# An attention kernel on one core: PSUM as four pairs of banks, keys and queries in alternating units, and a norm spread over steps

## The chip, the core and the metric

The kernel runs on one NeuronCore of a Trainium2 chip. A core has TensorE (PE: matmuls and, as PEld, weight loads), VectorE (DVE), ScalarE (ACT), GpSimd (POOL), and SyncE (SP), which here issues the DMAs. Matmuls write to PSUM[...]; DVE and ACT read PSUM and write to SBUF, the working memory. Each engine runs its own instructions in order and waits on semaphores for the others. The metric is the device time of one execution, in microseconds, as the median of several runs.

## What is computed

The input is 16 images of 64 x 64 positions with 256 channels, in fp32. There are two layers, each with a group norm over 32 groups of 8 channels ahead of it and a residual around it:

```python
# layer 0: linear attention over all positions of an image, 8 heads of 32
q, k, v = split(gn(x) @ w_qkv)
q = softmax(q, over the 32 channels of a head) * 32**-0.5
k = softmax(k, over all positions)
x = x + ((k.T @ v).T @ q per head) @ w_out
# layer 1: local attention in a 7 x 7 window, 8 heads of 32
q, k, v = gn(x) @ Wq + bq, gn(x) @ Wk + bk, gn(x) @ Wv + bv
scores = q . (k at each of the 49 neighbours + emb)    # emb: by row for heads 0-3, by column for 4-7
x = x + sum over neighbours of softmax(scores) * v
```

## The kernel before

**Layout.** An image is kept channels first, as two halves of 128 channels by 4096 positions. The positions are cut into eight strips of 512. Strips 1 to 7 are blocks of 8 columns by 64 rows, strip 0 holds the two borders of the image (5 columns on one side, 3 on the other). The tuple KEYED lists the strips with the border last, ORDER lists them as layer 0 visits them, and UNITS lists the four units of 16 columns that the local attention visits, unit 0 last. The 16 images follow each other in one program; each engine of TensorE, ACT, DVE and SP carries out its instructions in the order in which the Python code writes them.

**PSUM.** There are two double tiles of two banks (`double`, in the profile pd) and four single ones (`single`, ps); lines 366 to 387. `psum2` hands out the two doubles in turn, `bank` the first half of the next one. `banks` hands out, again in turn, double 0, double 1, singles 0 and 1, singles 2 and 3, with the engine that is to empty each of the two banks (0 is DVE, 1 is ACT).

**Layer 0** (`layer0`, line 515). For 16 pieces of 256 positions, queries and keys are made (L531), put through exp by ACT (L535), summed and transposed by DVE (L538, L562), and the context is accumulated in singles 0 and 1 (L549). At the end the context is multiplied by the output weights and with the queries (L642), two channel halves in turn; DVE adds the result to the image (L653, L656) and takes the statistics of the sum (L465).

**Preparing layer 1** (line 1023 on). `group_stats` turns statistics into mean and rstd in three steps, with two tiny matmuls that average over a group (L262 to L281). The weights are scaled with rstd (L668), and the mean is folded into the biases (`fold_bias`, and L1036 with L1039 for the values). `positional_products` (L695) and `positional` (evacuations L686 by DVE, L684 by ACT) make the products of queries with the position embedding; `store_rings` and `load_rings` bring them through DRAM into rows of the query tile qq. `values` (line 734) makes the values of one strip: eight matmuls (L743), an add of the bias by DVE (L746), a store to the scratch vpad in DRAM (L751; the border, L756, takes eight DMAs). After the last strip `load_window` (L804, four DMAs each) brings the values of the first two units back, as windows.

**Keys and queries** (`keys_queries`, line 760). This is done for the first four heads (hg 0) and, after their local attention, for the others (hg 1); I call each a half of the layer. First the keys of four pairs of strips in the order of KEYED, (2,3), (4,5), (6,7), (1,0), then the queries of the same pairs. Each pair takes eight matmuls (L771) into two banks, and each strip is evacuated one head at a time, by 32 x 512 instructions (for the border 32 x 320 and 32 x 192), keys into kaug, queries into qq. The queries of (1,0) are held back by a `yield`: they are made in the first step of the local attention.

**Local attention** (`local_attention`, line 807) goes through 20 groups (four units with five groups of at most two chunks of keys) in 24 steps. At its start four tiny matmuls (L951) write to all four banks of the doubles. A step makes the scores of its group (L834, into a double from `psum2`), whose exp ACT writes to work tiles (L843 for hg 0, L846 for hg 1); it multiplies the exps of the group of the step before with the values (`weighted`, L878, into singles 0 and 1, `outs`), and sums those of the group before that (`summed`, L908, into singles 2 and 3, `zs`). DVE adds the parts of neighbouring chunks (`both_chunks`, L863). When a unit is complete, ACT copies `outs` (L970), DVE transposes `zs` (L915) and inverts the sums in `finish`, POOL multiplies and adds to the image (L934, L942), SP stores.

**Between the steps** the callbacks `between0` and `between1` do the next image's work. Step n calls them with the group of step n - 2. In hg 1 `between1` starts the loads of the next image's first channel half after the first group, takes two strips' statistics (L465, DVE) after each of the first four groups of the second unit, makes the three steps of `group_steps` after the first three groups of the third unit (with the matmul of the mean in the score bank that comes next, `next_bank`), and normalises two strips (L285, two instructions each) after the second and third group of the last unit.

**Work tiles.** One pool of six buffers of 128 x 1024 serves layer 0's exps, the values before they are stored, and the exps of the scores, in turn.

## Time and profile before

| | |
|---|---|
| median of 3 runs | 5888.22 us |
| lowest, highest | 5876.85, 5892.97 us |
| the profiled execution, its own time | 5892.37 us |
| its span, first to last instruction | 5890.5 us |
| mean granted clock of TensorE | 0.954 |
| instructions | 169110 |

In the lines that follow, a row of the timeline gives start, length, engine, line, operation, output <- inputs with the shape, and the number of instructions that it merges; in brackets stands how long the engine had been idle before it, and what ended that. A row of the waits gives who waited for whom, the total in us, the number of times and the longest. A row of a group gives line, engine and operation, shape, count, then busy us and mean ns of one, then the idle time before them and what ended most of it. In the chain, shares are of the span. The time of one image is about 367 us: layer 0 and the preparation of layer 1 take some 165 of them, each half of layer 1 some 100.

### The profile page before, as it was taken

What the parts mean: (1) busy time and instruction counts of PE and PEld (TensorE: products, weight loads), DVE (VectorE), ACT (ScalarE), POOL (GpSimd) and SP (SyncE); (2) the same over time, 40 slices, a digit from 0 to 9 for tenths busy, and PEclk for the clock granted to TensorE, in tenths of its full rate; (3) what the DMA queues carried; (4) which work ended last, traced back from release to release, by engine and by line L of the source; (5) the groups of instructions that cost most, each with busy time, mean ns of one, the idle gap of its engine ahead of it and who ended that gap; (6) DMA issues with size and microseconds to landing.
All of it is one profiled execution on the core that took longest, in us unless ns stands there. A gap on an engine that the chain in (4) does not pass through costs nothing.

```text
span 5890.5 us, 169110 instructions
## 1 busy us (share of the span) xinstructions
PE 5235.4 (89%) x75313; PEld 3609.8 (61%) x75313; DVE 3439.0 (58%) x5946; ACT 2193.7 (37%) x3089; POOL 1335.2 (23%) x1946
## 2 busy tenths in 40 slices
PE   7889898898998989989889998988989989899997
PEld 4656566566665666656656666565665666656665
DVE  4565655656565565655655556565574655656555
ACT  1341624425144251442514325144351433514335
POOL 3031231302212022130221302213032130321303
PEclk9999999999999999999999999999999999999999
DMA  4543616445173451734517345173451734517344
GB/s 121 107 102 56 133 54 116 101 74 119 42 130 96 76 115 35 131 94 77 117 33 131 94 77 117 33 133 92 79 119 32 136 86 81 114 35 135 87 77 86
DMA packets 751604, 540.80 MB, mean 92 GB/s; under 512 B 241408, under 2 KB 682368, under 8 KB 748416
## 3 DMA queue, kind: packets, MB, share of 16 engines
q1 hardware_dynamic: 750864, 529.89, 44.1%
q8 instruction: 592, 9.70, 0.7%
q14 instruction: 148, 1.21, 0.1%
HBM read 371.04 MB, written 158.73 MB: 90 GB/s over the span
## 4 chain that ended last, share of the span: by engine, by line
PE 77%; DVE 8%; ACT 5%; issue 5%; DMA 2%; SPq 1%; POOL 1%; DVEq 0%; ACTq 0%; POOLq 0%
PE pd L531 15%; PE pd L834 13%; PE ps L878 8%; PE pd L771 7%; PE ps L549 6%; PE ps L771 5%; ACT qq L684 4%; PE ps L642 4%; PE pd L743 4%; PE pd L642 4%; PE ps L743 4%; PE ps L908 4%; DVE e L863 3%; PE ps L695 2%; DMA vpad<-v 1%
## 5 line engine op out<-in xcount | busy, mean ns | idle before, releaser
L863 DVE TENSOR_TENSOR e<-e,e 128x384 f32<-128x384 f32 x1024 | 732.4, 742 | 773.1 <-PE ps L878 615.2
L834 PE MATMUL pd<-qq,kaug 64*64 64x112 f32 (+4 forms) x27648 | 938.0, 277 | 159.8 <-issue 71.1
L834 PEld LDWEIGHTS pd<-qq,kaug 64*64 64x64 f32 x27648 | 813.2, 139 | 319.5 <-issue 181.8
L531 PE MATMUL pd<-wqkv,img 128*128 128x512 f32 x2048 | 948.8, 608 | 3.2 <-DVE img L285 3.2
L443 POOL TENSOR_TENSOR others<-others,rc 128x32 f32<-128x32 f32 x128 | 32.1, 251 | 2858.6 <-DVE rc L919 2858.4
L535 ACT ACTIVATE eq<-pd 128x1024 f32<-128x1024 f32 x256 | 261.9, 1023 | 1077.7 <-PE pd L531 1077.7
L531 PEld LDWEIGHTS pd<-wqkv,img 128*128 128x128 f32 x2048 | 399.1, 196 | 412.1 <-issue 376.6
L878 PE MATMUL ps<-e,vw 128*32 128x112 f32 (+1 forms) x18432 | 575.2, 261 | 65.2 <-issue 64.5
L538 DVE TENSOR_REDUCE qz<-eq 128x16 f32<-128x512 f32 x256 | 175.5, 686 | 766.9 <-ACT eq L535 766.9
L846 ACT ACTIVATE e<-pd 128x896 f32<-128x896 f32 (+2 forms) x576 | 461.4, 836 | 430.5 <-PE pd L834 423.5
L843 ACT ACTIVATE e<-pd 128x896 f32<-128x896 f32 (+2 forms) x576 | 462.4, 838 | 400.7 <-PE pd L834 395.8
L684 ACT ACTIVATE qq<-ps,bias 32x512 f32<-32x512 f32 (+2 forms) x512 | 318.6, 648 | 733.5 <-PE ps L695 668.6
L908 PE MATMUL ps<-e,ones 128*32 128x128 f32 (+2 forms) x10240 | 404.2, 266 | 146.3 <-DVE e L863 113.0
L878 PEld LDWEIGHTS ps<-e,vw 128*32 128x32 f32 x18432 | 419.0, 114 | 154.4 <-issue 117.5
L942 POOL TENSOR_TENSOR img<-img,r 128x320 f32<-128x320 f32 (+1 forms) x512 | 493.2, 993 | 0.0
L549 PE MATMUL ps<-xtok,eq 128*128 128x257 f32 x2048 | 483.4, 380 | 0.0
L549 PEld LDWEIGHTS ps<-xtok,eq 128*128 128x128 f32 x2048 | 387.4, 190 | 149.8 <-issue 107.1
L684 ACT ACTIVATE kaug<-pd,bias 32x512 f32<-32x512 f32 x256 | 173.7, 678 | 674.8 <-PE pd L771 671.9
L686 DVE TENSOR_SCALAR qq<-ps,bias 32x512 f32<-32x512 f32 (+2 forms) x416 | 312.3, 759 | 151.0 <-PE ps L771 145.2
L934 POOL TENSOR_TENSOR r<-r,r 128x512 f32<-128x512 f32 x256 | 340.7, 1352 | 140.5 <-DVE r L921 134.8
L908 PEld LDWEIGHTS ps<-e,ones 128*32 128x32 f32 x10240 | 253.3, 116 | 189.6 <-DVE e L863 148.1
L465 DVE BATCH_NORM_STATS2 st<-img 128x6 f32<-128x512 f32 x512 | 332.1, 679 | 9.7 <-DMA img<-in_xc 5.2
(128 smaller groups left out, 6609.9 us busy)
## 6 DMA issues: line engine op xcount, KB each, us to landing
vw<-vpad SPq DMA_DIRECT2D x512, 288.0 KB
img<-in_xc SPq DMA_DIRECT2D x256, 256.0 KB
xtok<-in_xt SPq DMA_DIRECT2D x64, 1024.0 KB
out<-img SPq DMA_DIRECT2D x256, 256.0 KB
vpad<-v SPq DMA_DIRECT2D x112, 512.0 KB
qq<-pos SPq DMA_DIRECT2D x128, 256.0 KB
qq<-in_ring SPq DMA_DIRECT2D x128, 256.0 KB
pos<-qq SPq DMA_DIRECT2D x128, 112.0 KB
```

What stands on the lines that cost most here:

```text
L531: nc.tensor.matmul(ps[:, t], xn[k][:, n0 : n0 + P], n.wqkv_sb[:, k, : 2 * C], start=(k == 0), stop=(k == 1))
L549: nc.tensor.matmul(pc[hg][:, : C + 1], eq[p][:, t, C + hg * P : C + (hg + 1) * P], xtok[p // 4][:, 2 * (p % 4) + t], start=(p == 0 and t = ...
L642: nc.tensor.matmul(py[a], w4[rows, h, hg, co * P : (co + 1) * P], qv[rows, 4 * hg + h, 8 * HD * i : 8 * HD * (i + 1)], start=(h == 0 and h ...
L684: nc.scalar.activation(dst, src, AF.Identity, bias=bias)
L743: nc.tensor.matmul(pi[:, t], x[k][:, n0 : n0 + P], wv[:, k], start=(k == 0), stop=(k == 1))
L771: nc.tensor.matmul(ps[a], wgt[:, k, hg * P : (hg + 1) * P], x[k][:, strip(pair[a])], start=(k == 0), stop=(k == 1),)
L834: nc.tensor.matmul(to, kaug[pl][rows, u, 8 * c : 8 * c + 8].rearrange("p r w -> p (r w)"), q, start=True, stop=True,)
L843: nc.scalar.activation(e.rearrange("p (a n) -> p a n", a=2), ps[:, :, : 2 * m], AF.Exp)
L863: nc.vector.tensor_tensor(part, part, rows_of(c - 1, before, r0, 8 * c), ALU.add)
L878: nc.tensor.matmul(dst, stationary, pr, **flags)
L908: nc.tensor.matmul(dst, ones, pr, start=True, stop=True)
L942: nc.gpsimd.tensor_tensor(yv, xv, by_rows(add[:, :, a - w0 : e - w0], xv), ALU.add)
```

## The change

The two double and four single tiles become four pairs of two banks each. `psum2` takes pairs 0 and 1 in turn, `outs` is pair 2 and `zs` pair 3, each emptied by one instruction (the copy by ACT, the transpose by DVE) in place of two. Layer 0's context uses the halves of pairs 2 and 3; both channel halves of its output are added by two wide DVE instructions. The values take the four pairs in turn and are evacuated by one add. The folds of the mean have banks of their own choice: pair 2 (second half), pair 1 (second half) and pair 1 (first half).

Keys and queries go by pairs of strips (0,1), (2,3), (4,5), (6,7), keys then queries of each pair; the pairs of banks are taken in turn, so that keys use pairs 0 and 2 and queries 1 and 3. DVE evacuates all keys, ACT all queries, except the last unit (queries of strips 6 and 7, behind the `yield`), whose heads are split between them. Where a pair holds no border, both strips go in one 32 x 1024 instruction for each head.

The windows of the first two units are loaded after the stores of strips 7 and 1, so one strip's store and the border's stand behind them on SP. For the next image's norm, `between1` takes one strip's statistics after each of eight groups from the fourth on, makes the steps of `group_steps` one group later than before, and normalises one half of one strip after each of the first four groups of the last unit. `group_steps` reads mean and variance where `bn_aggr` wrote them, without a copy.

The diff, cut; the old form of `keys_queries` and what only renames banks is left out:

```diff
--- before.py
+++ after.py
@@ -260,18 +261,16 @@
             nc.vector.bn_aggr(mv[:, k], stats[:, k].rearrange("p a b -> p (a b)"))
-        mean_c, var_c = mv[:, :, 0:1], mv[:, :, 1:2]
-        rhs = small.tile([P, 2, 1], F32, tag="gn1", name=f"gn1{name}")
-        nc.vector.tensor_copy(rhs, mean_c)
+        mean_c, var_c = mv[:, :, 0], mv[:, :, 1]
         yield
         pm = psum(f"pm{name}")
-        nc.tensor.matmul(pm[:, 0:2], self.grp, rhs.rearrange("p a b -> p (a b)"), start=True, stop=True)
+        nc.tensor.matmul(pm[:, 0:2], self.grp, mean_c, start=True, stop=True)
         mean = small.tile([P, 2], F32, tag="gnm", name=f"gnm{name}")
...
         d = small.tile([P, 2], F32, tag="gnd", name=f"gnd{name}")
-        nc.vector.tensor_tensor(d, rhs.rearrange("p a b -> p (a b)"), mean, ALU.subtract)
+        nc.vector.tensor_tensor(d, mean_c, mean, ALU.subtract)
         nc.vector.tensor_tensor(d, d, d, ALU.mult)
-        nc.vector.tensor_tensor(d, d, var_c.rearrange("p a b -> p (a b)"), ALU.add)
+        nc.vector.tensor_tensor(d, d, var_c, ALU.add)
         yield
...
@@ -363,28 +362,19 @@
 
-        double = [ps.tile([P, 2, 512], F32, tag=f"pd{i}", name=f"pd{i}") for i in range(2)]
-        single = [ps.tile([P, 512], F32, tag=f"ps{i}", name=f"ps{i}") for i in range(4)]
-        turn = [0, 0]
+        pairs = [ps.tile([P, 2, 512], F32, tag=f"pair{i}", name=f"pair{i}") for i in range(4)]
+        turn = [0]
 
...
             turn[0] += 1
-            return double[turn[0] % 2]
-
-        def banks():
-
-            i = turn[1] % 4
-            turn[1] += 1
-            if i >= 2:
-                return single[2 * i - 4 : 2 * i - 2], (0, 1)
-            return [double[i][:, j] for j in range(2)], (i, i)
+            return pairs[turn[0] % 2]
 
...
 
-            return double[(turn[0] + 1) % 2][:, 0, 64:]
+            return pairs[(turn[0] + 1) % 2][:, 0, 64:]
 
...
@@ -634,26 +624,22 @@
                 for co in range(2):
-                    py = [double[a // 2][:, a % 2, : 2 * P] if co else single[a][:, : 2 * P] for a in range(4)]
+                    py = [pairs[2 - 2 * co + a][:, :, : 2 * P] for a in range(2)]
                     for h in range(4):
...
                                 nc.tensor.matmul(
-                                    py[a],
+                                    py[a // 2][:, a % 2],
                                     w4[rows, h, hg, co * P : (co + 1) * P],
...
                     xv = x[co][:, s0 * 512 : (s0 + 2) * 512].rearrange("p (t a n) -> p a t n", a=4, n=HD)
-                    if co:
-                        for a in (0, 2):
-                            part = double[a // 2][:, :, : 2 * P].rearrange("p a (t n) -> p a t n", n=HD)
-                            nc.vector.tensor_tensor(xv[:, a : a + 2], part, xv[:, a : a + 2], ALU.add)
-                    else:
-                        for a in range(4):
-                            nc.vector.tensor_tensor(xv[:, a], py[a].rearrange("p (t n) -> p t n", n=HD), xv[:, a], ALU.add)
+                    for a in range(2):
+                        part = py[a].rearrange("p a (t n) -> p a t n", n=HD)
+                        nc.vector.tensor_tensor(xv[:, 2 * a : 2 * a + 2], part, xv[:, 2 * a : 2 * a + 2], ALU.add)
                     for s in (s0, s0 + 1):
...
@@ -733,17 +719,13 @@
 
-            pv, _ = banks()
+            pv = pairs[KEYED.index(s) % 4].rearrange("p i (t c) -> p (i t) c", c=C)
             v4 = work_tile(f"v4_{b}_{s}").rearrange("p (t c) -> p t c", c=C)
-            for i in range(2):
-                pi = pv[i].rearrange("p (t c) -> p t c", c=C)
-                for t in range(2):
-                    n0 = s * 512 + (2 * i + t) * P
-                    for k in range(2):
-                        nc.tensor.matmul(pi[:, t], x[k][:, n0 : n0 + P], wv[:, k], start=(k == 0), stop=(k == 1))
-            for i in range(2):
-                pi = pv[i].rearrange("p (t c) -> p t c", c=C)
-                nc.vector.tensor_tensor(v4[:, 2 * i : 2 * i + 2], pi, bv.unsqueeze(1).to_broadcast([P, 2, C]), ALU.add)
+            for t in range(4):
+                n0 = s * 512 + t * P
+                for k in range(2):
+                    nc.tensor.matmul(pv[:, t], x[k][:, n0 : n0 + P], wv[:, k], start=(k == 0), stop=(k == 1))
+            nc.vector.tensor_tensor(v4, pv, bv.unsqueeze(1).to_broadcast([P, 4, C]), ALU.add)
             v = vpad[b % 2]
...
@@ -759,38 +741,51 @@
+            for i in range(8):
+                pair, what = QUERIED[i // 2], i % 2
+                wgt = wq if what else wk
+                ps = pairs[i % 4]
+                if i == 7:
+                    yield
+                for a in range(2):
+                    for k in range(2):
+                        nc.tensor.matmul(
+                            ps[:, a],
+                            wgt[:, k, hg * P : (hg + 1) * P],
+                            x[k][:, strip(pair[a])],
+                            start=(k == 0),
+                            stop=(k == 1),
+                        )
+                for h in range(4):
+                    rows = slice(h * HD, (h + 1) * HD)
+                    d0 = 64 * (h % 2)
+                    keys, queries = kaug[h // 2][d0 : d0 + HD, :, PAD : PAD + W], qq[d0 : d0 + HD, h // 2]
+
+                    engine = h // 2 if i == 7 else i % 2
+                    b0 = bias[rows, 2 * what + hg : 2 * what + hg + 1]
+                    if pair[0]:
+                        u = pair[0]
+                        src = ps[rows]
+                        if not what:
+                            dst = keys[:, u : u + 2].rearrange("p u r w -> p u (r w)")
+                        else:
+                            w = 8 * u - PAD
+                            src = src.rearrange("p u (r w) -> p u r w", w=8)
+                            dst = placed(queries, hg)[:, :, w : w + 16].rearrange("p r (u w) -> p u r w", w=8)
+                            if hg:
+
+                                dst, src = (a.rearrange("p u r w -> p u w r") for a in (dst, src))
+                        evacuate(engine, dst, src, b0)
+                        continue
                     for a in range(2):
...
+                        for u, p0, m, w, view in pieces(pair[a]):
+                            src = view(ps[rows, a])
+                            dst = placed(queries, hg)[:, :, w : w + m] if what else keys[:, u, :, p0 : p0 + m]
+                            dst = by_rows(dst, src)
+                            if what and hg:
+                                order = "p r w -> p w r" if len(src.shape) == 3 else "p g r w -> p w g r"
+                                dst, src = dst.rearrange(order), src.rearrange(order)
+                            evacuate(engine, dst, src, b0)
 
...
@@ -909,10 +904,9 @@
 
-                for k in range(2):
-
-
-                    nc.vector.transpose(r[:, k], zs[k])
+
+
+                nc.vector.transpose(r, pairs[3])
                 yield
...
@@ -966,8 +960,7 @@
                         rs[i] = [tail.tile([P, 2, 512], F32, tag=f"tail{k}", name=f"r{b}_{hg}_{i}_{k}") for k in range(2)]
-                        for j in range(2):
-                            nc.scalar.copy(rs[i][1][:, j], outs[j])
+                        nc.scalar.copy(rs[i][1], pairs[2])
                         vw.pop(i)
...
@@ -1022,22 +1015,23 @@
                 scale(wpos, n.wpos, rstd)
-                pairs = [ORDER[i : i + 2] for i in range(0, NS, 2)]
-                positional_products(0, x, pairs[0])
-                pb = bank("fold")
+                scored = [ORDER[i : i + 2] for i in range(0, NS, 2)]
+                positional_products(0, x, scored[0])
+                pb = pairs[2][:, 1]
                 fold_bias(mean, wpos, (4,), pb)
...
                     if i < 3:
-                        positional_products(i + 1, x, pairs[i + 1])
-                    positional(i, pairs[i])
-                pv = bank("foldv")
+                        positional_products(i + 1, x, scored[i + 1])
+                    positional(i, scored[i])
+                pv = pairs[1][:, 1]
                 for k in range(2):
...
                 store_rings()
+                vw = {}
                 for i, s in enumerate(KEYED):
...
@@ -1045,10 +1039,12 @@
                         load_rings(0)
-                pb = bank("fold2")
+
+                    if i in (5, 6):
+                        vw[i - 5] = load_window(b, 0, UNITS[i - 5])
+                pb = pairs[1][:, 0]
                 fold_bias(mean, wk, (0, 1), pb)
                 fold_bias(mean, wq, (2, 3), pb)
-                vw = {i: load_window(b, 0, UNITS[i]) for i in range(2)}
                 if more:
...
@@ -1090,15 +1086,17 @@
                         load_half(b + 1, 0)
-                    if i == 1 and g < 4:
-                        for s in ORDER[2 * g : 2 * g + 2]:
-                            strip_stats(st, x_next, 0, s)
-                    if i == 2 and g == 0:
+
+                    at = 5 * i + g - 3
+                    if 0 <= at < NS:
+                        strip_stats(st, x_next, 0, ORDER[at])
+                    if at == NS:
                         steps = n.group_steps(st, 1e-5, small, next_bank, f"0_{b + 1}", gn)
-                    if i == 2 and g < 3:
+                    if NS <= at < NS + 3:
                         next(steps, None)
-                    if i == 3 and g in (1, 2):
-                        normalise(xn_next, x_next, *gn, ORDER[g - 1])
+                    if i == 3 and g < 4:
+                        k, o = g % 2, strip(ORDER[g // 2])
+                        n.normalise(xn_next[k][:, o], x_next[k][:, o], *gn, k)
 
...
```

## The prediction

> **What bounds the kernel now.** I read the page's busy shares first, then the chain of work that ended last, then the waits, then the timeline of one image (image 8, 2954.8 to 3325.5 us), then the instruction groups with their shapes kept apart.
>
> ```profile
> PE 5235.4 (89%) x75313; PEld 3609.8 (61%) x75313; DVE 3439.0 (58%) x5946; ACT 2193.7 (37%) x3089; POOL 1335.2 (23%) x1946
> ...
> PE 77%; DVE 8%; ACT 5%; issue 5%; DMA 2%; SPq 1%; POOL 1%; DVEq 0%; ACTq 0%; POOLq 0%
> PE pd L531 15%; PE pd L834 13%; PE ps L878 8%; PE pd L771 7%; PE ps L549 6%; PE ps L771 5%; ACT qq L684 4%; PE ps L642 4%; PE pd L743 4%; PE pd L642 4%; PE ps L743 4%; PE ps L908 4%; DVE e L863 3%; PE ps L695 2%; DMA vpad<-v 1%
> ```
>
> TensorE (PE) is the bound. The change removes no matmul, so it can only fill the 11% in which PE is idle and the time in which its clock is halved (the granted clock is 0.954 on average). ACT qq L684 stands in the chain with 4%: there PE waits for a ScalarE evacuation of queries. The list of waits gives its size:
>
> ```profile
> PE pd L951 <- ACT qq L684: 55.5, 27, 2.4
> ...
> PE pd L834 <- ACT e L843: 30.6, 16, 1.9
> PE pd L834 <- ACT e L846: 28.8, 16, 1.8
> ```
>
> The first one comes at the start of each of the 32 half layers (5 more of these waits, 11.8 us, are put down to a DMA): the initialisation of the score banks needs the bank from which ACT still evacuates queries of strips 4 and 5. The other two, one in each half, come two steps later, when the score banks wait for exps that are queued on ACT behind the border's queries. Together 67.3 + 59.4 = 126.7 us, 4.0 us a half. The timeline of image 8 shows both, and what follows:
>
> ```profile
> 3147.98 0.39 PE L951 MATMUL pd<-bits,nb 32*128 32x512 bf16 x2
> 3150.72 0.39 PE L951 MATMUL pd<-bits,nb 32*128 32x512 bf16 x2 [2.35 <-ACT qq L684]
> 3152.55 5.21 PE L771 MATMUL ps<-img,wqn 128*128 128x512 f32 x8
> 3157.80 3.45 ACT L684 ACTIVATE qq<-ps,bias 32x320 f32<-32x320 f32 x8 [2.67 <-PE ps L771]
> 3162.24 2.74 PE L834 MATMUL pd<-qq,kaug 64*64 64x112 f32 x48 [1.92 <-ACT e L843]
> ```
>
> The eight matmuls at 3152.55 take 5.21 us, where eight take 3.43 undisturbed. The table of windows says why (columns: length, busy time of PE, PEld, DVE, ACT, POOL, PE clock, DMA):
>
> ```profile
> 3148.79:3152.21 3.42, 1.49 (x49) 1.26 (x49) 1.55 (x3) 3.34 (x6) 0.00 (x0) 1.00 1.18 219
> 3152.21:3155.62 3.41, 3.41 (x15) 1.67 (x8) 0.00 (x0) 2.88 (x4) 0.00 (x0) 0.50 0.66 241
> ```
>
> A window in which PE was busy 1.49 of 3.42 us is followed by one at half clock. Windows with idle stretches of 1.33 and 1.39 us (busy 2.07 and 2.01 of 3.40) were not.
>
> [...] 128x384 to 128x896 exps cost 0.492 and 0.922 us (0.84 ns an element), and L656 to L653, 128x256 to 128x512 from PSUM, 416 and 686 ns (1.05).
>
> **The change, part by part.**
>
> *Keys and queries.* The rows used:
>
> ```profile
> L686 DVE TENSOR_SCALAR kaug<-pd,bias 32x512 f32<-32x512 f32 x256 | 191.2, 747 | 78.4 <-PE pd L771 75.2
> L684 ACT ACTIVATE qq<-pd,bias 32x512 f32<-32x512 f32 x256 | 181.7, 710 | 65.0 <-PE pd L771 62.2
> ```
>
> No row shows a 32x1024 evacuation. Bounds: the 512 row alone (nothing for the rest, 0.71 ACT, 0.75 DVE) and twice that (1.42, 1.49). I take the 512 row plus 512 elements at the slopes: ACT 0.71 + 0.43 = 1.14, DVE 0.75 + 0.54 = 1.29. A unit of two strips is then 4 x 1.14 = 4.6 us on ACT (now 8 x 0.71 = 5.7) and 5.2 on DVE (now 6.0).
>
> Count from the first L771 of a half. A unit takes PE 3.43 us; its evacuation starts about 0.3 later. The order is K01, Q01, K23, Q23, K45, Q45, K67 and, after the first scores, Q67. ACT: Q01 (4 x 0.71 + 4 x 0.55 + 4 x 0.39 = 6.6) from 7.2 to 13.8, Q23 14.0 to 18.6, Q45 20.9 to 25.5. DVE: K01 (3.0 + 2.6 + 1.8 = 7.4) 3.7 to 11.1, K23 to 16.3, K45 17.4 to 22.6, K67 24.3 to 29.5. No bank is late: K45 wants pair 0 at 13.7, Q45 pair 1 at 17.1, K67 pair 2 at 20.6. DVE's 22.9 us of keys lie under PE's 24.0. PE is through K67 at 24.0, initialises pair 0 to 24.35, waits for pair 1 to 25.55 (1.2 instead of 2.35), starts the scores at 25.9 (before: 27.3), Q67 27.4 to 30.8. ACT's half of Q67 is 2 x 1.14, 31.1 to 33.4, in place of 3.45; the next exps end at 34.3 and 35.3; PE asks for the banks at 33.4, so the second wait is 1.0 instead of 1.9. The scores of the fourth step start at 37.6. Layer half 2, where ACT is a little quicker (5.52 for 8): 37.2.
>
> In the trace of before the same stretch, read at the fifteen images whose two halves can be told apart, means 41.1 and 40.8 us, and 39.6 and 39.0 where no half clock falls in it. So waits are worth 2.0 and 1.8 us a half (cross-check: 4.0 of waits now, 2.0 left), half clock another 1.5 and 1.8. Idle stretches of 1.2 and 1.0 lie under the 1.39 that left the clock alone; I keep a quarter of the half-clock loss for windows in which another stall adds up. Sum: 16 x (3.5 + 3.6) = 114, less 16 x 0.8 = **101 us**.
>
> *Values.* The add of bv reads the bank that the first values want, in every second image:
>
> ```profile
> 3092.73 1.56 PE L743 MATMUL pd<-wvn,img 128*128 128x256 f32 x6 [2.46 <-DVE bvn L1039]
> ```
>
> Gap from L1036 to L743: 0.97 us in odd images, 3.3 in even ones, since the two double banks alternate. In the change the fold sits in pair 1 and the first values in pair 0, which DVE has evacuated by 3088.4. The second strip's values, in pair 1, want the add of bv at 3093.4, when it is done (3092.7). So 8 x 2.4 = **19 us**. One evacuation of 1024 in place of two is 0.1 us of DVE under 3.45 of PE: nothing.
>
> *Windows ahead of border stores.* Eight loads pass one strip's and the border's stores on SP's queue. The loads leave some 10 us earlier, the eight border stores 7.6 us later, landing near 3150. Who waits: the value tile of the border is the slot that the sixth exp of the half wants, at K start + 36, here 3155 or later. 5 us to spare: nothing (bounds: the 11.8 us of waits put down to this DMA as a gain, rival 3 as a loss). Not moving them would not have been free, since scores now come sooner: DMA is busy up to 3154, and the weighted products need the window by K start + 33.
>
> *Norm.* The copy L265 (0.17 us uncontended) falls out of the path to the second layer's weights: 16 x 0.2 = **3 us**. For the next image's norm: hg 1 from its fourth step to the next image takes 60.8 us on average, hg 0 from there to the next keys 55.5, with the same matmuls. Some 5 us a norm are DVE's: pairs of L465 (1.27) and L285 (up to 2.16 beside POOL) ahead of both_chunks, and the matmul of the mean in a score bank. One a step lets the first fit between (some 1.5 us less wait in steps 7 to 10, 0.75 at the end), but the mean's copy stays behind DVE adds [...], and steps 5, 6, 11 and 12 get an L465 that they had not. I take 2.5 of 5, bounds -1.5 and 5: 15 x 2.5 = **38 us**.
>
> *Single evacuations of outs and zs*, two wide adds for four (1.42 to 1.29): they hide under PE (L642 runs without a gap at 3.45); if not, 0.06 us x 128 = 8 us.
>
> Sum: 101 + 19 + 3 + 38 = 161 us. The profiled execution took 5892.37 us (span 5890.5), 4 above the median 5888.22; it would become 5731, the median **5727**.
>
> **The rivals.**
> 1. *The evacuation stays the bound*: a 32x1024 costs twice a 32x512. Q45 ends at 26.6, the exps a further 0.6 later, PE's idle stretch passes 2 us and the half clock stays. Left of the 101 are about 32: 32 + 19 + 3 + 38 = 92, or 5796. Against it: both slopes above. 0.15. If besides the strided write of the last queries holds back the scores that follow until it ends (3 us a half), a wait takes the place of the one removed, and nothing measurable is left (5880): 0.06.
> 2. *More*: no half clock is left and the norm costs nothing: 114 + 19 + 3 + 15 x 5 = 211: 5677; were a 32x1024 as cheap as its lower bound, the waits would shrink by some 2 us more a half (64 us), the far end. 0.14.
> 3. *Slower, 5936*: SP stands at a window load until stores have landed, and the border's stores behind it come so late that ACT stands at the sixth exp. Each us past the spare 5 costs one; with 10 us of gains in each image it decides from 15 us. At 18 it costs 16 x 3 = 48. For it: SP's queue is dense from 3092 to 3147. Against it: SP shows no wait of L804 on vpad today, directly behind the last store. 0.06.
>
> **How the numbers follow.** The forecast has 0.59, own range 5690 to 5775. With rivals 1 and 2: 5650 to 5815 leaves less than 2 in 10 out. About 0.3% (18 us) is what a measurement can tell from no change. Faster: 0.59 + 0.15 + 0.14 = 0.88. Same 0.06. Slower 0.06.
>
> **What would show it.** Right: L951's wait near 1.1 us, first scores 25.9 us after the first key matmul, 32x1024 rows at 1.14 (ACT) and 1.29 (DVE), no gap ahead of L743, mean clock above 0.96. Wrong: 32x1024 rows near 1.42; half clock still behind the first scores; a wait of DVE for img from in_xc in steps 5 to 8; exps that wait for vpad's stores; PE waiting for the mean's copy as long as now (1.6 to 1.8).

## The result, and the profile after

The changed kernel takes 5926.88 us (median of 20 runs, 5903.48 to 5947.98) where the kernel before, run beside it, takes 5880.22 (20 runs, 5844.36 to 5912.85). The ratio is 1.0067, interval 1.0053 to 1.0082: about 0.7% slower. The forecast was 5727 us, a gain of 2.7%, and its range ended at 5815.

The profiled execution of the changed kernel took 5903.48 us (span 5901.7), at the quick end of its runs; that of before 5892.37 (span 5890.5). The two traces therefore show 11 us of a difference that is 47 us between the medians and 39 by the ratio. What they can show is where gains and losses cancelled. The page's first line says that TensorE is as busy as it was, and that the other two engines have less to do:

```profile
PE 5247.3 (89%) x75313; PEld 3620.3 (61%) x75313; DVE 3409.1 (58%) x5338; ACT 2001.3 (34%) x2385; POOL 1354.6 (23%) x1946
```

DVE lost 608 instructions and ACT 704, and ACT's busy time fell from 2193.7 to 2001.3 us. The groups with their shapes kept apart have the new evacuations:

```profile
L672 DVE TENSOR_SCALAR kaug<-pair,bias 32x1024 f32<-32x1024 f32 x384 | 491.5, 1280 | 134.0 <-PE pair L752 129.8
...
L670 ACT ACTIVATE qq<-pair,bias 32x1024 f32<-32x1024 f32 x320 | 373.9, 1168 | 278.6 <-DVE qq L672 172.9 <-PE pair L752 102.9
```

1.28 and 1.17 us: the forecast had 1.29 and 1.14, so its slopes were right and rival 1 is out. The last entry of the second line is what no forecast had. ACT idled 172.9 us ahead of its evacuations of queries because of DVE's evacuations of queries. The list of waits shows the same, and what became of the two waits that the forecast was about:

```profile
ACT qq L670 <- DVE qq L672: 172.9, 32, 5.4
...
PE pair L829 <- ACT e L838: 60.3, 17, 3.7
PE pair L829 <- ACT e L841: 54.9, 16, 3.4
...
PE pair L945 <- ACT qq L670: 33.4, 32, 1.3
```

The first wait (L945, the initialisation) shrank as forecast, from 67.3 us to 33.4. The second (L829, scores for exps) was to fall from 59.4 to about 32; it grew to 115.2. There are 32 waits of ACT for DVE, one for each half layer. Half of the 5.4 us is time before PE had made these queries; what DVE adds shows in the timeline of image 8, just after its first scores:

```profile
3172.95 2.57 DVE L672 TENSOR_SCALAR qq<-pair,bias 32x1024 f32<-32x1024 f32 x2 [1.82 <-issue]
...
3175.61 2.47 ACT L670 ACTIVATE qq<-pair,bias 32x1024 f32<-32x1024 f32 x2 [5.41 <-DVE qq L672]
3178.11 1.73 ACT L838 ACTIVATE e<-pair 128x896 f32<-128x896 f32 x2
...
3179.08 2.89 PE L829 MATMUL pair<-qq,kaug 64*64 64x112 f32 x48 [3.67 <-ACT e L838]
```

DVE evacuates heads 0 and 1 of the last queries (two instructions, 2.57 us); ACT, which had nothing else to do, begins heads 2 and 3 only 0.09 us after DVE has ended; its exps are queued behind them; and PE stands 3.67 us. The table of windows (length, busy time of PE, PEld, DVE, ACT, POOL, PE clock, DMA) shows what the stall cost on top:

```profile
3175.21:3178.62 3.41, 0.20 (x10) 0.00 (x0) 0.87 (x2) 2.97 (x3) 0.00 (x0) 1.00 0.02 5
3178.62:3182.03 3.41, 2.95 (x52) 2.75 (x56) 0.00 (x0) 2.13 (x3) 0.00 (x0) 0.50 0.00 0
```

A window in which PE was busy 0.20 of 3.41 us, and after it one at half clock. So the half clock that the forecast meant to remove stayed, and grew. The table has the stretches of an image, read from both traces as means of the fifteen images that have a next one. In the first two rows the forecast holds no half clock; it kept a loss of 0.8 us an image for both together, which stands in the third row as 1.7 us at half clock, since at half clock a matmul of 128x512 takes 0.85 us in place of 0.43, so that half of such a stretch is lost:

| stretch, us | before | forecast | after |
| --- | --- | --- | --- |
| first key matmul to fourth-step scores, layer half 1 | 41.12 | 37.6 | 42.72 |
| the same, layer half 2 | 40.78 | 37.2 | 41.95 |
| of both, at half clock | 7.3 | 1.7 | 12.7 |
| values' fold to first values | 2.20 | 1.0 | 0.97 |
| fourth-step scores of half 2 to the next image | 60.77 | 58.3 | 57.86 |
| start of the image to the values' fold | 136.72 | 136.5 | 138.31 |

### The profile page after: what moved, and what is told of

Same layout as the page of the kernel before. It is cut to its first block, busy times and chain, and to the rows that moved or that the text cites. A ratio compares the mean times of both kernels' runs of the same rounds, so it can differ in the third digit from the quotient of the medians.

```text
span 5901.7 us, 167950 instructions
## 1 busy us (share of the span) xinstructions
PE 5247.3 (89%) x75313; PEld 3620.3 (61%) x75313; DVE 3409.1 (58%) x5338; ACT 2001.3 (34%) x2385; POOL 1354.6 (23%) x1946
## 3 DMA queue, kind: packets, MB, share of 16 engines
q14 instruction: 140, 1.15, 0.1%
## 5 line engine op out<-in xcount | busy, mean ns | idle before, releaser
L670 ACT ACTIVATE qq<-pair,bias 32x1024 f32<-32x1024 f32 (+3 forms) x832 | 679.7, 847 | 1633.4 <-PE pair L681 671.9
L829 PE MATMUL pair<-qq,kaug 64*64 64x112 f32 (+4 forms) x27648 | 950.7, 280 | 206.3 <-issue 66.0
L829 PEld LDWEIGHTS pair<-qq,kaug 64*64 64x64 f32 x27648 | 827.0, 140 | 362.2 <-issue 177.5
L521 PE MATMUL pair<-wqkv,img 128*128 128x512 f32 x2048 | 952.8, 611 | 6.3 <-DVE img L284 6.3
L672 DVE TENSOR_SCALAR kaug<-pair,bias 32x1024 f32<-32x1024 f32 (+3 forms) x768 | 689.0, 922 | 217.4 <-PE pair L752 211.7
L873 PE MATMUL pair<-e,vw 128*32 128x112 f32 (+1 forms) x18432 | 572.3, 261 | 61.1 <-issue 60.6
L525 ACT ACTIVATE eq<-pair 128x1024 f32<-128x1024 f32 x256 | 262.2, 1024 | 1074.0 <-PE pair L521 1074.0
L838 ACT ACTIVATE e<-pair 128x896 f32<-128x896 f32 (+2 forms) x576 | 464.6, 836 | 442.7 <-PE pair L829 368.5
L841 ACT ACTIVATE e<-pair 128x896 f32<-128x896 f32 (+2 forms) x576 | 463.9, 835 | 425.8 <-PE pair L829 410.0
L752 PE MATMUL pair<-img,w 128*128 128x512 f32 x1024 | 484.4, 618 | 0.0
L539 PE MATMUL pair<-xtok,eq 128*128 128x257 f32 x2048 | 483.4, 380 | 0.0
L752 PE MATMUL pair<-img,wqn 128*128 128x512 f32 x1024 | 463.7, 595 | 0.0
```

The costliest lines, as they stand in the source:

```text
L521: nc.tensor.matmul(ps[:, t], xn[k][:, n0 : n0 + P], n.wqkv_sb[:, k, : 2 * C], start=(k == 0), stop=(k == 1))
L539: nc.tensor.matmul(pc[hg][:, : C + 1], eq[p][:, t, C + hg * P : C + (hg + 1) * P], xtok[p // 4][:, 2 * (p % 4) + t], start=(p == 0 and t = ...
L670: nc.scalar.activation(dst, src, AF.Identity, bias=bias)
L672: nc.vector.tensor_scalar(dst, src, bias, None, ALU.add)
L752: nc.tensor.matmul(ps[:, a], wgt[:, k, hg * P : (hg + 1) * P], x[k][:, strip(pair[a])], start=(k == 0), stop=(k == 1),)
L829: nc.tensor.matmul(to, kaug[pl][rows, u, 8 * c : 8 * c + 8].rearrange("p r w -> p (r w)"), q, start=True, stop=True,)
```

## The experiments

Three theories could explain the result. **Shared tile**: the last unit of queries is split by rows between DVE and ACT, and the two take turns in the pair of banks; ACT's turn comes second, and its exps come late. **New order**: the order of units (keys and queries in turn) makes the exps late by itself. **Small waits**: folds that moved into shared pairs cost more than was saved. Each run below is given as a ratio to the kernel before, timed beside it. Times given for stretches are from the traces, read as in the table above.

**The last queries on VectorE alone.** `engine` is 0 for the last unit:

```diff
-                    engine = h // 2 if i == 7 else i % 2
+                    engine = 0 if i == 7 else i % 2
```

> The changed kernel, with the last unit of queries evacuated by VectorE alone (4 x 32x1024 at 1.28 us, 5.1 us), so that no bank is read by two engines. Theory (sharing a bank delays the exps): ScalarE has nothing of the last unit, the exps start when their scores are done, the second wait falls from 3.5 us to below 0.5 us, no half clock follows; first key matmul to fourth-step scores 36.5 to 37.5 us, 16 x (5.5 + 5) = 170 us at most, of which I expect 90 to 150 to reach the end: 5785 to 5845 where the kernel before takes 5880 (ratio 0.984 to 0.994). Rival (the order of units is the cause): near the changed kernel, ratio 1.005 to 1.01. Rival (VectorE becomes the bound: its additions of overlapping rows queue behind 5.1 us of queries): the exps are on time but the row sums of the third step wait for VectorE; ratio about 1.0.

Measured: 5792.34 us, ratio 0.9832 (0.9808 to 0.9855). One expression in the code moves the time by 2.3%, from 0.7% slower than before to 1.7% faster. The same place of image 8:

```profile
3109.85 5.17 DVE L672 TENSOR_SCALAR qq<-pair,bias 32x1024 f32<-32x1024 f32 x4 [1.81 <-issue]
3110.71 1.73 ACT L838 ACTIVATE e<-pair 128x896 f32<-128x896 f32 x2 [3.60 <-PE pair L829]
...
3112.24 1.56 PE L829 MATMUL pair<-qq,kaug 64*64 64x112 f32 x48
```

DVE's share has doubled, and yet all is sooner: ACT is free, its exps wait for nothing but their scores, and the scores of PE follow without a wait. First key matmul to fourth-step scores fell to 38.17 and 37.84 us, 0.3 to 0.7 above what I expected, since half clock in the two stretches did not vanish but fell from 12.7 to 3.1 us. The order of units is the change's own here, and the loss is gone: the new-order theory is out. DVE as the new bound cost little; PE waits for its queries at the row sums 11.7 us in all:

```profile
PE pair L903 <- DVE qq L672: 11.7, 32, 0.4
```

**The last queries shared by strip.** If what is held is a bank, then giving DVE the bank of strip 6 and ACT the bank of strip 7 sets both free:

```diff
-                    engine = h // 2 if i == 7 else i % 2
+                    engine = i % 2
-                    if pair[0]:
+                    if pair[0] and i < 7:
...
-                            evacuate(engine, dst, src, b0)
+                            evacuate(a if i == 7 else engine, dst, src, b0)
```

> The changed kernel, with the last unit of queries (strips 6 and 7) shared by strip: VectorE evacuates the bank of strip 6 and ScalarE the bank of strip 7 (4 x 32x512 each), where the changed kernel shares each bank by rows. [...] If what is held is a bank, ScalarE runs beside VectorE, from first key matmul to fourth-step scores takes about 38 us instead of 42.7 and 42.0, and the whole is 80 to 110 us below the changed kernel, about 50 us below the kernel before (ratio 0.991). If what is held is the pair of banks (the whole tile), ScalarE still waits some 3 us for VectorE and the time stays near that of the changed kernel (ratio to before 1.005 to 1.012). Rival, that the delay comes from the new order of units and not from the sharing: also 1.005 to 1.01, but without a wait of ScalarE for VectorE.

Measured: 5974.42 us, ratio 1.0143 (1.0121 to 1.0166): worse than the change, and above the 1.005 to 1.012 that I expected if the whole pair is held. The two engines, now each in a bank of its own, hand the pair to and fro. The waits, and the timeline:

```profile
ACT qq L670 <- DVE qq L672: 190.7, 128, 3.5
...
DVE qq L672 <- ACT qq L670: 74.6, 96, 0.8
```
```profile
3196.54 0.74 DVE L672 TENSOR_SCALAR qq<-pair,bias 32x512 f32<-32x512 f32 x1 [1.81 <-issue]
3197.31 0.74 ACT L670 ACTIVATE qq<-pair,bias 32x512 f32<-32x512 f32 x1 [3.52 <-DVE qq L672]
...
3198.08 0.75 DVE L672 TENSOR_SCALAR qq<-pair,bias 32x512 f32<-32x512 f32 x1 [0.81 <-ACT qq L670]
```

Eight evacuations run strictly one after the other, though no two neighbours of them touch one bank. So it isn't the bank that is held.

**The same with two tiles.** The fourth pair is declared as two tiles of one bank; engines and order of the last queries stay as in the run above:

```diff
-        pairs = [ps.tile([P, 2, 512], F32, tag=f"pair{i}", name=f"pair{i}") for i in range(4)]
+        pairs = [ps.tile([P, 2, 512], F32, tag=f"pair{i}", name=f"pair{i}") for i in range(3)]
+        last = [ps.tile([P, 512], F32, tag=f"last{i}", name=f"last{i}") for i in range(2)]
```

(and its users take the two in turn, with two instructions where the pair had one).

> The kernel in which the last queries are shared by strip, one bank to each engine, with one thing different: the fourth pair of banks is declared as two tiles of one bank each in place of one tile of two banks (its evacuations are 32x512 and 128x512 for that reason). Theory: what one engine keeps from another is the tile, as the program orders its accesses, and not the bank; then ScalarE no longer waits for VectorE, first key matmul to fourth-step scores falls from 44.1 and 43.7 us to 38.5 to 39.5, and the time from 1.014 to 0.988 to 0.994 of the kernel before. Rival: VectorE and ScalarE cannot read two neighbouring banks at once in the hardware, or wait for another reason: ratio stays 1.005 to 1.015, with waits of ScalarE for VectorE as before.

Measured: 5782.68 us, ratio 0.9843 (0.9819 to 0.9867), from 1.0143. In image 8:

```profile
3104.86 3.70 PE L768 MATMUL last<-img,wqn 128*128 128x512 f32 x8
...
3106.94 3.04 DVE L678 TENSOR_SCALAR qq<-last,bias 32x512 f32<-32x512 f32 x4
...
3108.60 3.02 ACT L676 ACTIVATE qq<-last,bias 32x512 f32<-32x512 f32 x4 [2.69 <-PE last L768]
...
3111.65 1.73 ACT L854 ACTIVATE e<-pair 128x896 f32<-128x896 f32 x2
3112.62 1.70 PE L845 MATMUL pair<-qq,kaug 64*64 64x112 f32 x48 [1.50 <-ACT e L854]
```

DVE from 3106.94 to 3109.98, ACT from 3108.60 to 3111.62: side by side, 0.76 us for each instruction, where they took 0.74 to 0.76 by turns. ACT waits for its matmuls only. The stretches are 38.10 and 38.16 us. Both engines write to the same tile qq and read the same biases in both runs, so it is not these that were held. What was held is the **tile** that they read: the program orders accesses of two engines by the tile that was declared, reads after reads too, and a pair declared as one tile is held whole. With tiles of one bank DVE also starts when the first bank's matmuls are done, at 3106.94, while PE still fills the second.

**The sharing alone, in the kernel before**, whose last queries lie in two one-bank tiles:

```diff
-                                evacuate(engines[a], dst, src, bias[rows, 2 * what + hg : 2 * what + hg + 1])
+                                engine = h // 2 if what and i == NS - 2 else engines[a]
+                                evacuate(engine, dst, src, bias[rows, 2 * what + hg : 2 * what + hg + 1])
```

> The kernel before, with one thing of the change alone: its last queries (strips 1 and 0, the border) shared by rows, heads 0 and 1 by VectorE and heads 2 and 3 by ScalarE, each in both banks, in place of one engine for each bank. Each engine's work is about the same as now. Theory (two engines in a bank wait for each other): ScalarE starts only after VectorE has left the first bank, the exps come 1 to 2 us later in each of the 32 halves, and more half clock follows: 30 to 70 us slower (ratio 1.005 to 1.012). Rival (reads of one bank by two engines run side by side): within 10 us of the kernel before, or a little faster, since the border's pieces are then split evenly.

Measured: 5898.73 us, ratio 1.0012 (0.9997 to 1.0026). My expectation of 30 to 70 us was wrong. The wait is there, and it hardly counts:

```profile
ACT qq L684 <- DVE qq L686: 76.4, 64, 3.9
...
PE pd L835 <- ACT e L844: 34.0, 17, 2.1
PE pd L835 <- ACT e L847: 32.8, 16, 2.1
```

ACT does wait for DVE, in a bank whose other rows it wants, once for each bank. But with a tile for each bank it can start on the first while DVE is in the second; and the even split gives back a little of what the wait takes (ACT's share of this unit is 1.50 + 1.72 us in image 8, where it was 3.45). The scores' wait for exps grew by only 66.8 - 59.4 = 7.4 us. Set beside the change, this suggests that the damage needed two things: two engines in one tile, and a tile so large that the first engine's whole share lies in it. The two kernels differ in more than that, so the second is argued from these lines and not shown alone.

**Windows loaded late**, with the last queries on VectorE alone: the two loads go back behind the border's stores.

```diff
-                vw = {}
...
-                    if i in (5, 6):
-                        vw[i - 5] = load_window(b, 0, UNITS[i - 5])
...
                 fold_bias(mean, wq, (2, 3), pb)
+                vw = {i: load_window(b, 0, UNITS[i]) for i in range(2)}
```

> The changed kernel with the last queries on VectorE alone, and the first two windows of values loaded where the kernel before loads them, after the values and behind the border's stores. Theory (the forecast's nothing, as long as the stores are not late): within 10 us of the same kernel with the early loads, ratio 0.981 to 0.985. Rival: with the scores 3 us sooner the first products wait for the window: 1 to 3 us an image, ratio 0.985 to 0.991.

Measured: 5793.92 us, ratio 0.984 (0.9819 to 0.9861), the same as 0.9832 with the early loads. The two intervals span about 0.2% to either side, so no worth of the move can be told, and the rival's mechanism isn't seen; the forecast's sentence that leaving the loads would not have been free isn't borne out.

**The norm alone, in the kernel before** (the spread over steps, and the means read in place):

```diff
...
-                    if i == 1 and g < 4:
-                        for s in ORDER[2 * g : 2 * g + 2]:
-                            strip_stats(st, x_next, 0, s)
+                    at = 5 * i + g - 3
+                    if 0 <= at < NS:
+                        strip_stats(st, x_next, 0, ORDER[at])
...
```

> The kernel before, with the spread of the next image's norm and without the copy of the means, the change's other parts left out. The traces show 2.9 us less from the second half's fourth step to the next image, 15 times, and the forecast had 2.5 x 15 + 3: 40 to 47 us below the kernel before (ratio 0.992 to 0.993). Rival (the stretch is only shorter because the scores before it came later, so that statistics had more time): within 15 us of the kernel before.

Measured: 5876.62 us (22 runs), ratio 0.9981 (0.9968 to 0.9995): 11 us, between 3 and 19, and not 40 to 47. In the trace the stretch of half 2 fell from 60.77 to 59.48 us, 1.3 an image. That is little beside what one trace can tell: two of the kernels below, whose code is the same in this stretch, have 59.26 and 59.84. The time at half clock in the stretch fell from 9.3 to 4.8 us an image, and half of that, 2.2 us, is more than the gain, while PE's idle time in it fell only from 12.0 to 11.6; so this gain is at least in part clock. The mean's matmul still holds a score bank. PE's wait for the mean's copy, first in the kernel before, then here:

```profile
PE pd L834 <- DVE gnm L270: 21.0, 15, 2.1
```
```profile
PE pd L832 <- DVE gnm L268: 18.9, 15, 1.5
```

**Another turn of the pairs**, on top of the last queries on VectorE: the units take pairs 1, 3, 2, 0, 1, 3, 2, 3, so that the two pairs that the scores want first are those of the fourth and fifth unit.

```diff
+TURNS = (1, 3, 2, 0, 1, 3, 2, 3)
...
-                ps = pairs[i % 4]
+                ps = pairs[TURNS[i]]
```

> The changed kernel with the last queries on VectorE alone, and the eight units of keys and queries in pairs 1, 3, 2, 0, 1, 3, 2, 3 in place of 0, 1, 2, 3, 0, 1, 2, 3, so that the two pairs which the scores want first have been evacuated by then (their last units are the fourth and the fifth). Theory: the first wait, 1.3 us a half and 32 us in all, goes with nothing in its place; the first scores come 25.6 us after the first key matmul instead of 26.9 and 26.6, and the whole takes 25 to 45 us less than with the last queries on VectorE alone: ratio 0.976 to 0.980. Rival: the last queries now wait for the pair of the sixth unit, or the first products for the pair of the seventh, and the gain is lost there: ratio 0.982 to 0.986.

Measured: 5792.58 us, ratio 0.9833 (0.9811 to 0.9855): no gain, as with the rival, but by a wait that I had not named. The initialisation no longer waits, but the first scores need the queries themselves that ACT is still writing. First the wait with the old turn of pairs, then the one with the new:

```profile
PE pair L945 <- ACT qq L670: 32.1, 31, 1.3
```
```profile
PE pair L830 <- ACT qq L671: 17.2, 32, 0.8
```

Half of the 32 us came back as this wait, in place of the bank it is the data. The other half was not seen in the time either: the fourth-step scores came 0.6 us sooner in half 1 and 0.1 in half 2, and the trace, which is of the slowest of these five runs, is longer elsewhere, by 0.7 us an image ahead of the values' fold and 0.3 from the first values to the keys, with more half clock in an image (29.2 us, from 26.9). Why there isn't shown.

**The folds moved**, on top of that:

```diff
-            pv = pairs[KEYED.index(s) % 4].rearrange("p i (t c) -> p (i t) c", c=C)
+            pv = pairs[(KEYED.index(s) + 1) % 4].rearrange("p i (t c) -> p (i t) c", c=C)
...
-                pv = pairs[1][:, 1]
+                pv = pairs[0][:, 1]
...
-                pb = pairs[1][:, 0]
-                fold_bias(mean, wk, (0, 1), pb)
-                fold_bias(mean, wq, (2, 3), pb)
+                    if i == 6:
+                        fold_bias(mean, wk, (0, 1), pairs[1][:, 0])
+                        fold_bias(mean, wq, (2, 3), pairs[2][:, 0])
```

> The kernel with the other turn of pairs, and the two small folds put where their pair is free: the fold for the values' bias into pair 0 (ScalarE does not evacuate from it), the values from pair 1 on, and the folds for the keys' and queries' biases after the seventh strip's values, into two pairs. Theory: 0.54 us ahead of the values' fold and 0.8 us at the end of the values return in each image, and fewer key stages begin at half clock: 16 x 1.3 = 21 us, up to 35 with the clock; ratio 0.972 to 0.976. Rival: the values' first strip then waits for ScalarE in pair 1 instead, and the 0.8 us are hidden by another wait: within 10 us of the kernel with the other turn of pairs.

Measured: 5742.12 us, ratio 0.9771 (0.9747 to 0.9795), 0.6% below the run before it: 36 us by the ratios, where the theory gave 21 to 35. In the changed kernel the second fold waits for the first one's bias, which stands on DVE behind the last add of the values, and in 6 of the 16 images the keys after it, those of half 1, fell to half clock within their first eight matmuls. First the changed kernel at image 8, then this one:

```profile
3139.35 0.65 PE L663 MATMUL pair<-gnm,wqn 128*64 128x1 f32 x16 [0.80 <-DVE bias L665]
3139.93 5.40 PE L752 MATMUL pair<-img,w 128*128 128x512 f32 x8
```
```profile
3049.39 3.60 PE L753 MATMUL pair<-img,w 128*128 128x512 f32 x8
```

Eight matmuls in 5.40 us there, in 3.60 here; none of the 16 images has half clock there now.

**The old norm in this kernel**: statistics by two, norm and normalising where they were (the diff of the norm alone, reversed, but with the means still read in place).

> The kernel with the other turn of pairs and the moved folds, with the next image's statistics, means and first normalised strips where the kernel before has them (the copy of the means stays out). It asks what the spread of the norm is worth where the scores are early. If it is the 1.2 to 1.3 us an image that the kernel with the spread alone showed in its trace: 18 to 20 us slower than the same kernel with the spread, ratio 0.979 to 0.982. If it is the forecast's 2.5 us: 38 us, ratio 0.983 to 0.985. If nothing: 0.976 to 0.978.

Measured: 5747.03 us, ratio 0.9771 (0.9744 to 0.9797), equal to the kernel with the spread. Here the spread shows no gain; the 18 us of the first case lie just inside what the two intervals leave open. In the traces the stretch of half 2 is 59.26 us with the spread and 59.85 without.

**The transposes of the context in another pair**, with the spread again: the matmuls L593 (L594 in this kernel) wrote into the second bank of the tile from whose first bank DVE was still copying.

```diff
-                        other[0][:, (2 * k + hg) * P : (2 * k + hg + 1) * P], cc[:, hg, k * P : (k + 1) * P], n.ident
+                        pairs[0][:, 0, (2 * k + hg) * P : (2 * k + hg + 1) * P], cc[:, hg, k * P : (k + 1) * P], n.ident
...
-                nc.vector.tensor_scalar(dst, other[0][:, k * C : (k + 1) * C], rstd[:, k : k + 1], None, ALU.mult)
+                nc.vector.tensor_scalar(dst, pairs[0][:, 0, k * C : (k + 1) * C], rstd[:, k : k + 1], None, ALU.mult)
```

> The same kernel (other turn, moved folds, spread norm) with the transposes of the context in the first pair of banks, so that the matmuls which read their first copied half no longer write into the tile from which VectorE still copies the second half. Theory (a matmul into one bank of a tile waits for reads of its other bank): the start of these matmuls comes 0.3 to 0.5 us sooner in each image, 5 to 9 us in all; ratio 0.975 to 0.977. Rival: the step after waits for VectorE anyway, within 3 us of the same kernel.

Measured: 5731.1 us, ratio 0.9726 (0.9698 to 0.9754), a little below what I expected. The wait with the folds moved, and now:

```profile
PE pair L594 <- DVE ct L589: 16.0, 16, 1.0
```
```profile
PE pair L594 <- DVE ct L589: 9.7, 16, 0.6
```

That is 6 us, and 9.7 is what the kernel before has too. Beside the old-norm run on the same chip this kernel took 16 us less, though their intervals overlap. The traces say where more than the 6 us may come from. In the seven runs with the longer wait (the change among them) they hold 3.0 to 5.0 us of half clock in an image from the last context to the end of layer 0's output; in the six with the shorter wait (the kernel before, the sharing and the norm alone in it, the two tiles, and the last two) 1.6 to 2.5.

**The second strip normalised last**, on top of that:

```diff
-                    if i == 3 and g < 4:
-                        k, o = g % 2, strip(ORDER[g // 2])
-                        n.normalise(xn_next[k][:, o], x_next[k][:, o], *gn, k)
+                    if i == 3 and g < 2:
+                        n.normalise(xn_next[g][:, strip(ORDER[0])], x_next[g][:, strip(ORDER[0])], *gn, g)
+                    if i == 3 and g == 4:
+                        normalise(xn_next, x_next, *gn, ORDER[1])
```

> That kernel with the norm's last two steps moved: the second strip is normalised after the last row sums have been released, not ahead of VectorE's last additions for them. In the trace PE waits 1.55, 0.94 and 0.92 us for these additions at the end of an image, with normalising instructions of 1.35, 0.96 and 0.53 us between them. If that is what is left of the norm's cost: 15 x 0.5 to 1.0 = 8 to 15 us less, ratio 0.972 to 0.975. If the additions are late for their own reasons (POOL beside them), within 4 us.

Measured: 5715.36 us, ratio 0.9709 (0.9682 to 0.9737), the fastest of all: 2.9% below the kernel before, and by the two ratios (0.9709 / 1.0067) 3.6% below the change. The stretch of half 2 fell by 0.66 us an image, from 59.84 to 59.18, which is 10 of the 16 us between the two medians. But the intervals of these two runs overlap, and a trace with the code of the first of them in this stretch had 59.26; so whether this last step gained anything isn't shown.

## Why the prediction was wrong, point by point

**The step that failed** is this one: "ACT's half of Q67 is 2 x 1.14, 31.1 to 33.4, in place of 3.45; the next exps end at 34.3 and 35.3; PE asks for the banks at 33.4, so the second wait is 1.0 instead of 1.9." Its length was right (2.47 us for two), its start was not. It has ACT begin when PE is done, side by side with DVE; on the chip ACT begins when DVE is done, 2.6 us later, and the second wait was 3.5 us. That two engines would be side by side in one tile was the author's estimate, and no row of the trace of before stood behind it: in that kernel no unit of keys and queries had two engines in one tile, which is visible in its code: a double tile had one engine, and where a unit had two engines, each had a single bank. This program orders by tile, also where the two engines want different rows (heads 0 and 1, heads 2 and 3: the list has 172.9 us of waits of ACT for DVE) or different banks (190.7 us in the run that shares by strip). No run here had two engines at once in one bank, which would need the wait itself gone and wasn't tried, so whether that costs anything isn't shown; two engines at once in two neighbouring banks cost nothing that the two-tile run shows (0.76 us each, beside 0.74 to 0.76 by turns).

With this step put right the time would have lain in the forecast's range: the kernel with the last queries on VectorE took 5792 us, inside 5650 to 5815, though still above 5727. What else was off follows.

**Keys and queries**, forecast 101 us: the change lost 16 x (42.72 - 41.12 + 41.95 - 40.78) = 44. With the last queries in a tile for each engine's share it would have been 16 x (3.02 + 2.62) = 90, with VectorE alone 16 x (2.95 + 2.94) = 94. So the rest of the step was sound: slopes, the first wait (33.4 us in all, 1.04 a half, 1.3 where it comes first; forecast 1.2), the first scores (26.4 to 26.8 us; forecast 25.9), the half clock that goes with the stalls. What is missing to 101 in the two-tile run are first scores 0.3 and 0.7 us later than forecast (26.2 and 26.6) and a second wait of 1.5 and 1.2 us in place of 1.0; the half clock left there, 1.7 us an image, is what I had kept. The two-tile run's second waits are

```profile
PE pair L845 <- ACT e L854: 23.9, 16, 1.5
...
PE pair L845 <- ACT e L857: 19.6, 16, 1.2
```

**Values**, 19 us: right, 16 x (2.20 - 0.97) = 20.

**Norm**, 38 us: too large, and the gain lay elsewhere. I took 2.5 of 5 us an image, though the two gains that I named, 1.5 and 0.75, make 2.25 before anything is taken off; alone the spread gave 1.3 in the trace (11 us of time), and in the kernel with moved folds none that could be measured. From scores to next scores, with the forecast's numbering of steps (from 0), the spread alone gave 0.6 us in steps 7 to 10, where the forecast had 1.5; steps 5, 6, 11 and 12 took 0.9 back; the end gave 0.4, where the forecast had 0.75; and steps 13 to 15, among them steps of the means in both kernels, gave 1.3, a gain that the forecast had not named. The sign that I had named for this came: in the change PE waits for the mean's copy as long as before (21.0 us):

```profile
PE pair L829 <- DVE gnm L269: 20.5, 15, 1.5
```

The 2.9 us that the changed kernel's trace shows in this stretch are more than the spread's own 1.3; that the rest is owed to the late scores, which give DVE's statistics room, is only argued; with the scores on time the stretch was longer again, 59.62.

**Edits costed at nothing or not at all**: the evacuations of values, outs and zs, and the windows, were nothing, as forecast. But from the image's start to the values' fold 1.6 us were lost, 25 us in all, most of it through pairs that two users share where each had a tile: the fold waits until ACT has left the other bank of its pair (0.52 us from the last positional matmul to it became 1.06), the context's matmuls wait for both copies of DVE (6.52 us from the last context to the output became 7.07), and the output itself lengthened by 0.3, which is half clock: 2.5 us of it lie in the output in place of 1.7, and less the half of that the output takes 28.5 and 28.6 us. At the end of the values the second fold waits 0.8 where it waited 0.3. The fold's wait, which the kernel before does not have, and the context's, which was 9.7 there:

```profile
3109.21 1.13 PE L1029 MATMUL pair<-wvn,gnm 128*128 128x256 f32 x4 [0.46 <-ACT qq L670]
```
```profile
PE pair L593 <- DVE ct L588: 15.9, 16, 1.0
```

The forecast read these lines for their gains and did not ask who else was in the tile.

**The sum** of the changed kernel's trace: -44 + 20 + 15 x 2.9 - 25 - 3 (values to keys, 0.2 an image) = -8 us, where the spans differ by -11. With the last queries on VectorE alone: 94 + 20 + 15 x 1.15 - 16 x 1.39 = 109, less 7 that two other stretches lost (values to keys 0.21, half 1 after its fourth step 0.25 us an image): 102, where 99 were measured. The forecast's three rivals didn't hold: the evacuations cost what I took, the gain was not larger, and moving the loads past the stores changed nothing that could be told. A slower end did come, by a fourth mechanism: the one unit that is shared by rows, which the forecast had priced without its wait.

**The clock.** In the changed kernel's trace half clock comes 111 times, 53 times for 3.41 us, 55 times for 6.83 and three times for longer, always at a granted 0.50. What goes before it doesn't give a rule. Half clock followed the window of 0.20 us busy above, but also the six windows of the changed kernel that hold the 0.8 us stall ahead of the keys, in each of which PE is busy 2.62 of 3.41 us; and other windows of the same trace with 1.55 to 1.77 us busy were followed by full clock. So the forecast's reading that idle stretches under 1.39 us leave the clock alone does not hold, and what decides isn't shown here. What the runs add is leverage: in the change the two stretches after the keys hold 12.7 us at half clock an image, with VectorE alone 3.1. Since at half clock at most half of the length is lost (0.85 us a matmul in place of 0.43), up to 4.8 of the 8.7 us an image that this edit brought in the two stretches are clock; the rest is the wait itself.

## What to carry to other kernels

Before two buffers are made one, list for each declared tile which engines touch it and when: in this program a tile is held whole, by readers against readers, whatever banks or rows they use (the waits of ACT for DVE come to 172.9 us where their rows differed, 190.7 where their banks did). In such a program, split the work of a last unit by tiles, not by rows, or give it whole to the engine that has nothing urgent queued behind it; a longer evacuation on VectorE was far cheaper here than half of one that kept ScalarE's exps waiting behind it, and as cheap as two halves in two tiles (ratios 0.9832 and 0.9843). And cost the start of a shared step apart from its length: here the length was right and the start 2.6 us off.

## What the runs showed that was not expected

- Two engines' alternate reads of one pair of banks cost about 0.03 us a handover beside the reads (0.81 us of waiting for a read of 0.74 to 0.75), so the loss is the lost overlap, not the handover.
- A wait that is gone may only have hidden the next: with the initialisation free, the first scores waited for the queries themselves, 17.2 us where the initialisation had waited 32.1.
- A stall of 0.8 us ahead of a long run of matmuls cost more than itself: in 6 of 16 images the keys then ran partly at half clock, and their first eight matmuls took 5.40 us in place of 3.60.
